# Attention and gated feed-forward on one core: softmax denominators summed by accumulating DMAs, and one PSUM bank for projections and transposes

## The chip, the cores and the metric

The kernel runs on one NeuronCore of a Trainium2 chip. Its engines are TensorE (PE in the profile: matrix products, with the loading of weights shown apart as PEld), VectorE (DVE), ScalarE (ACT), GpSimd (POOL) and SyncE (SP, which only starts transfers here). They run side by side and wait for each other through semaphores; each works through its own queue in order. Sixteen DMA engines move data; a transfer is started from the queue of SP, ACT or POOL. PE writes to PSUM, eight banks of 2 KB per partition, which ScalarE and VectorE read; everything else lies in SBUF or in HBM. The metric is the device time of the whole program in microseconds (us).

## The reference, cut to what matters

The input x has 4 batches of 1024 rows of 512 floats. Two layers follow each other, each with a layer norm before and after:

```python
x = x + layernorm(attention(layernorm(x)))
x = x + layernorm(ffn(layernorm(x)))

def attention(x):                       # 16 heads of 32
    kqv = x @ Wqkv + bqkv               # named q, k, v in this order
    scores = einsum('bsnh,btnh->bnst', k, q) / sqrt(32)
    scores = triu(scores) - 10000 * tril(ones, -1)
    attn = softmax(scores, axis=2)
    out = einsum('bnkq,bknh->bqnh', attn, v)
    return out.reshape(b, s, 512) @ Wo + bo

def ffn(x):                             # 2048 hidden units, int32 weights less 128, scaled per row
    return (silu(x @ Wg.T) * (x @ Wu.T)) @ Wd.T
```

A masked score is -10000, not minus infinity, and the scores are normalised over axis 2. For each query the kernel needs the maximum, the sum of exponentials (the denominator), and the sum of exponentials times values.

## The kernel before, in words

The first part of the program is attention, the second the feed-forward layer (`ffn`), which is not changed except for what is loaded ahead of it.

**Steps, tiles, periods.** Heads are taken four at a time (a block, `hb`, of 128 columns), queries 512 at a time (`g`, 0 or 1). One `(b, hb, g)` is a *step*; there are 32. A step goes over its key tiles `c` of 128 keys: four for `g` = 0, eight for `g` = 1. The last four tiles of a step lie on the diagonal, and only 512, 384, 256 and 128 queries of them count. Each key tile is a *period* of the big loop (from line 756), 192 in all, plus a lead of 12 in which the maxima of the first steps are found.

**A period.** PE's order is written out by hand. In period `p` the loop emits, for each half `u` (two heads), the scores of tile `now` (`weights`, L350 and L358 into `st`; ScalarE's exponential into `pT`, L375; on the diagonal GpSimd's mask, L377) and the maxima of a tile 12 periods ahead (`maxima`: PE into `sc`, L265; VectorE's L273 and L277). Between the halves stand, for the tile before: the accumulating transfers (`add_up`), one entry of a list called `later` (GpSimd's and VectorE's small products of steps already done), and `values` (L394), which multiplies `pT` with the values into `po` and with ones into `pd`, the denominators. Then comes one piece of a list called `whole`, or else one piece of a projection; at the period's end `fill` adds more projections.

**The planner.** Projections (`project`: q, k and v, four pieces each of 256 rows, and `project_out`) wait in lanes with a cost, a due period and a condition; `rate` and `spare` spread them over the periods. `whole` holds unsplit pieces: `rows` (`shift_rows`, which transposes the maxima into `pm`, and `masked_part`, which makes the masked keys' share in `pb` and `t1`), `ln` (stages of the layer norm) and `turn` (`turn_v`: transposes of v into `pv`).

**Denominators.** For `g` = 1 (but not the last step), the tiles 0 to 4 are added in SBUF: tile 0's `pT` is the sum tile, and each next is added to it by an accumulating DMA from GpSimd's queue (L421, two of 512 KB, one per half). The sum and the three narrow tiles 5 to 7 are multiplied by ones near the end of the step. For `g` = 0, each of the four tiles is multiplied by ones.

**PSUM.** `ps_st` has one buffer of two banks for scores, `ps_big` two buffers of two banks for maxima, for the second half of the scores where both halves are emitted together, and for every projection and transposition, `ps_acc` one bank each for `po` and `pd`: eight banks.

**Layer norm and emptying.** `ln_stage` loads, measures, normalises and transposes one row tile a stage; `xnT` holds a whole batch, double-buffered, and projections wait for all of it. ScalarE empties `xt` (L482), `pq` (L496, L499), `pm` (L305) and `pb` (L315); VectorE empties `pv` (L509) and `py` (L531) and adds the denominators (L446).

Of the kernel before, what the change touches and what calls it, by code (L numbers as in the profile page):

```python
# [27 lines left out]
def tile_attn_ffn_sandwich(  # L28
# [70 lines left out]
    with ExitStack() as actx:  # L99
# [3 lines left out]
        pxn = pctx.enter_context(tc.tile_pool(name="a_xn", bufs=2))  # L103
# [8 lines left out]
        ppt = right("a_pt", 6)  # L112
# [8 lines left out]
        )  # L121

# [103 lines left out]
        for step in steps:  # L226
            at[step] = n_periods
            n_periods += 4 * (step[2] + 1)
        LEAD = 12
        state = {}  # L230
        later = []

# [62 lines left out]
        def shift_rows(step):  # L295

            b, hb, g = step
            w = wide[g % 2]
            pm = ps_big.tile([P, 4, P], BF16, tag="big", name=f"pm_{b}_{hb}_{g}")
            for jj in range(4):  # L300
                nc.tensor.transpose(
                    pm[:, jj, :], w[:, jj].rearrange("p h d -> p (h d)"), ident_bf
                )
            mT = p2.tile([P, 512], BF16, tag="mT", name=f"mT_{b}_{hb}_{g}")
            nc.scalar.copy(mT, pm.rearrange("p j n -> p (j n)"))  # L305
            state["mT", step] = mT

        def masked_part(step):
# [3 lines left out]
            pb = ps_big.tile([P, 512], F32, tag="big", name=f"pb_{b}_{hb}_{g}")  # L312
            nc.tensor.matmul(pb, lhsT=sel, rhs=mT, start=True, stop=True)
            t1 = e2.tile([P, 512], F32, tag="t1", name=f"t1_{b}_{hb}_{g}")
            nc.scalar.activation(t1, pb, AF.Exp, bias=masked)  # L315
# [14 lines left out]
            later.extend((counts, shared))  # L330
            state["extra", step] = t1, t2

        def summed(step):

            return step[2] > 0 and step != steps[-1]

        def weights(step, c, halves):
# [27 lines left out]
            for u in halves:  # L365


                to_sum = summed(step) and c == 0
                pT = (p2 if to_sum else ppt).tile(
                    [P, 2, 512], F32, tag="sum" if to_sum else "pT",  # L370
                    name=f"pT_{b}_{hb}_{g}_{c}_{u}",
                )
                if to_sum:
                    state["sum", step, u] = pT
# [6 lines left out]
                state["pT", step, c, u] = pT  # L381

        def values(step, c):
            b, hb, g = step
            v = state["vt", b, hb]
            n = 512 * (g + 1) - max(c * P, 512 * g)
            first, last = c == 0, c == 4 * g + 3
            if first:
                for t in ("po", "pd"):
                    state[t] = ps_acc.tile([P, 512], F32, tag=t, name=f"{t}_{b}_{hb}_{g}")  # L390

            def product(t, pT, n, start, stop):
                for h in range(HPB):
                    nc.tensor.matmul(  # L394
                        state[t][h * D : (h + 1) * D, 512 - n :],
                        lhsT=v[:, c, h * D : (h + 1) * D] if t == "po" else ones,
                        rhs=pT[h // 2][:, h % 2, :n],
                        start=start,
                        stop=stop,
                    )  # L400

            pT = [state["pT", step, c, u] for u in range(2)]
            if not summed(step):
                product("pd", pT, n, first, last)
            product("po", pT, n, first, last)
            if summed(step) and c > 4 * g:

                waiting = state.setdefault(("pd", step), [])
                waiting.append((pT, n))
                if c > 4 * g + 1:  # L410
                    if c == 4 * g + 2:
                        total = [state.pop(("sum", step, u)) for u in range(2)]
                        waiting.insert(0, (total, 512))
                    for k, (t, n) in enumerate(waiting):
                        product("pd", t, n, c == 4 * g + 2 and k == 0, last)
                    waiting.clear()

        def add_up(step, c, u):

            if summed(step) and 0 < c <= 4 * step[2]:  # L420
                nc.gpsimd.dma_start(  # L421
                    state["sum", step, u], state["pT", step, c, u], accum_op=ALU.add
                )

        def finish(step):
# [6 lines left out]
            t1, t2 = state.pop(("extra", step))  # L432
            if step == steps[-1]:
# [12 lines left out]
            nc.vector.tensor_tensor(t2, state["pd"], t2, ALU.add)  # L446
            nc.vector.tensor_tensor(t1, state["po"], t1, ALU.add)

# [26 lines left out]
        def ln_turn(b, j):  # L475
            if j == 0:
                state["xnT", b] = pxn.tile([P, HC, S], F32, tag="xnT", name=f"xnT_{b}")
            xn = state.pop(("xn", b, j))
            pt = ps_big.tile([P, HC, P], F32, tag="big", name=f"xt_{b}_{j}")
            for c in range(HC):  # L480
                nc.tensor.transpose(pt[:, c, :], xn[:, ts(c, P)], ident)  # L481
            nc.scalar.copy(state["xnT", b][:, :, ts(j, P)], pt)  # L482

        def project(b, hb, which, q):

            xnT = state["xnT", b]
# [5 lines left out]
            pq = ps_big.tile([P, 256], F32, tag="big", name=f"pq_{b}_{hb}_{which}_{q}")  # L492
            by_columns(pq, [(w_in[which, hb][:, c, :], xnT[:, c, ts(q, 256)]) for c in range(HC)])
# [7 lines left out]
        def turn_v(b, hb, half):  # L501
# [4 lines left out]
            pv = ps_big.tile([P, 4, P], F32, tag="big", name=f"pv_{b}_{hb}_{half}")  # L506
            for i in range(4):
                nc.tensor.transpose(pv[:, i, :], vT[:, ts(4 * half + i, P)], ident)
            nc.vector.tensor_copy(state["vt", b, hb][:, 4 * half : 4 * half + 4, :], pv)  # L509
# [11 lines left out]
        def project_out(b, j, half):  # L521
# [5 lines left out]
            py = ps_big.tile([P, 256], F32, tag="big", name=f"py_{b}_{j}_{half}")  # L527
# [32 lines left out]
        def load_raw(k, which):  # L560
            raw = []
            for what, src in zip(which, weight_blocks(k)):
                shape = [P, IB // P, H] if what == "d" else [P, HC, IB]
                pool = pre["stage_d" if what == "d" else "stage"]
                t = pool.tile(shape, I32, tag=f"raw_{what}", name=f"raw_{what}{k}")
                nc.sync.dma_start(t, src)
                raw.append(t)
            return raw

        def ffn_begin():  # L570
# [11 lines left out]
            pre["stage_d"] = actx.enter_context(tc.tile_pool(name="a_raw", bufs=1))  # L582
            for i in range(GT):
                nc.sync.dma_start(pre["rows"][:, i, :], x2[0, i * P : (i + 1) * P, :])
            pre["raw"] = load_raw(0, "gud")
# [4 lines left out]
        def ffn_stage(i):  # L590
# [3 lines left out]
            if i > 0:  # L594
                xn = state.pop(("xn2", i - 1))
                pt = ps_big.tile([P, HC, P], F32, tag="big", name=f"xt2_{i - 1}")
                for c in range(HC):
                    nc.tensor.transpose(pt[:, c, :], xn[:, ts(c, P)], ident)
                hi, lo = (pre[k][:, :, ts(i - 1, P)] for k in ("hi", "lo"))
                nc.scalar.copy(hi, pt)  # L600
                nc.vector.tensor_tensor(lo, pt, hi, ALU.subtract)  # L601
# [4 lines left out]
            if i < 3:  # L606
                k = "gud"[i]
                nc.vector.tensor_scalar_add(pre[k], pre["raw"][i], -ZERO_POINT)
            if i == 3:
                pre["raw"] = load_raw(1, "gu")  # L610

        def check_weights():

            pf = ps_big.tile([P, P], F32, tag="big", name="pf")
# [36 lines left out]

        def turn_piece(b, hb, half):
# [420 lines left out]
```

## Time and profile before

| | |
|---|---|
| Time, median of 3 runs | 1977.89 us (1974.43 to 1981.7) |
| The profiled execution | 1978.49 us, its span 1976.4 us |
| Granted TensorE clock, mean over the span | 0.991 |
| First and last product of `values` | 80.4 and 1234.5 us |
| In 81 to 1235 us, busy | PE 1096.8, VectorE 797.5, ScalarE 442.0, GpSimd 426.2 us |
| Accumulating transfers | 120 of 512 KB, median 5.9 us from issue to landing |

How to read the profile's rows: a group is named by its line, engine, operation and `out<-in`; then come the shape, the count after `x`, the busy time and mean length of one, and the idle time of the engine before it with what ended it. In a row of the waits, "A <- B: total, times, longest" says how long A stood still until B ended. A timeline row gives start and length in us, and the idle time before it in brackets. A float32 product is recorded as two matmuls, so the four heads of one `pd` group are eight. The ends of matmuls are modelled and overlap the next start; what a group takes is read from start to start. In the slices, each digit is the busy share of a fortieth of the span in tenths, and PEclk the granted clock.

### The profile page before, as it was taken

How to read it: one execution, taken by the hardware profiler on the slowest of the kernel's cores; microseconds unless marked ns; L12 is line 12 of the kernel's file. 1: busy time of each engine (PE TensorE's matmuls, PEld its weight loads, DVE VectorE, ACT ScalarE, POOL GpSimd, SP SyncE). 2: the span in 40 equal slices, each digit the busy share in tenths (PEclk: the TensorE clock that was granted, in tenths of full speed). 3: DMA queues.
4: the chain of work that ended last, by engine and by line, in shares of the span. 5: the costliest groups of instructions: out<-in, count | busy, mean ns of one | idle time of the engine just before them, and what ended most of it. 6: DMA issues, size and time to landing. Idle time of an engine off the chain costs nothing.

```text
span 1976.4 us, 42103 instructions
## 1 busy us (share of the span) xinstructions
PE 1889.4 (96%) x18241; PEld 1121.0 (57%) x18241; DVE 1171.8 (59%) x1913; ACT 643.3 (33%) x962; POOL 524.3 (27%) x896
## 2 busy tenths in 40 slices
PE   7999999999999999999999989999999999999997
PEld 4444444444443444444444434688888888888886
DVE  4678777786675677675666773554344444444444
ACT  2244344434423434423344323122222222222221
POOL 2134233243343244344233344201010101101011
PEclk9999999999999999999999999999999999999999
DMA  3164255344235144144144351531010101001000
GB/s 113 55 145 100 68 121 126 77 118 97 50 87 114 27 98 92 39 103 92 23 87 86 98 129 50 175 108 43 1 44 0 43 6 38 32 11 43 0 22 23
DMA packets 65633, 137.56 MB, mean 70 GB/s; under 512 B 6304, under 2 KB 20640, under 8 KB 65440
## 3 DMA queue, kind: packets, MB, share of 16 engines
q0 software_dynamic: 17280, 62.92, 17.2%
q1 hardware_dynamic: 41008, 67.40, 10.1%
q10 hardware_dynamic: 7152, 4.46, 0.7%
q8 instruction: 145, 2.38, 0.5%
q14 instruction: 48, 0.39, 0.1%
HBM read 55.07 MB, written 16.78 MB: 36 GB/s over the span
## 4 chain that ended last, share of the span: by engine, by line
PE 82%; DVE 10%; ACT 4%; issue 2%; POOL 2%; DMA 1%; DVEq 0%; POOLq 0%; ACTq 0%; SPq 0%
PE pq L237 16%; PE pg L915 11%; PE pu L915 11%; PE acc L948 11%; PE sc L265 8%; PE po L394 5%; PE py L237 4%; PE st L350 4%; PE pd L394 4%; PE st L358 3%; DVE nm L277 3%; ACT pT L375 3%; DVE vl L516 2%; DVE sc L273 1%; PE xt L481 1%
## 5 line engine op out<-in xcount | busy, mean ns | idle before, releaser
L375 ACT ACTIVATE pT<-st 128x1024 f32<-128x1024 f32 (+3 forms) x384 | 310.2, 811 | 406.5 <-PE st L358 307.6
L277 DVE TENSOR_REDUCE nm<-sc 128x2 f32<-128x1024 f32 (+3 forms) x384 | 367.2, 957 | 117.5 <-PE st L358 98.2
L237 PE MATMUL pq<-xnT,w 128*32 128x256 f32 x6144 | 373.7, 386 | 16.1 <-DVE nm L277 6.8
L265 PE MATMUL sc<-in,in 32*128 32x512 f32 (+3 forms) x1536 | 347.8, 537 | 13.3 <-DVE nm L277 13.0
L237 PEld LDWEIGHTS pq<-xnT,w 128*32 128x32 f32 x6144 | 188.4, 111 | 218.4 <-issue 48.2
L358 PE MATMUL st<-in,in 32*128 32x512 f32 (+3 forms) x1536 | 308.7, 490 | 0.0
L925 DVE SCALAR_TENSOR_TENSOR h<-pu,pre_us,s 128x512 f32<-128x512 f32 x128 | 96.1, 750 | 312.8 <-PE pu L915 309.9
L377 POOL TENSOR_SCALAR_AFFINE_SELECT pT<-pT 128x256 f32<-128x256 f32 x256 | 113.5, 445 | 446.4 <-ACT pT L375 445.8
L948 PE MATMUL acc<-d,h 128*128 128x512 f32 x896 | 224.8, 393 | 0.2 <-DVE h L935 0.2
L273 DVE TENSOR_TENSOR sc<-sc,bound 128x256 f32<-128x256 f32 x256 | 109.2, 426 | 169.3 <-PE sc L265 96.6
L948 PEld LDWEIGHTS acc<-d,h 128*128 128x128 f32 x896 | 166.1, 188 | 34.2 <-DVE h L935 0.5
L923 ACT ACTIVATE s<-pg,pre_gs 128x512 f32<-128x512 f32 x128 | 88.1, 688 | 274.8 <-PE pg L915 274.7
L394 PE MATMUL po<-pT,vt 128*32 128x512 f32 (+3 forms) x1536 | 166.5, 502 | 1.0 <-POOL pT L377 1.0
L934 ACT CAST h<-h 128x512 fp32r<-128x512 f32 x128 | 79.5, 621 | 247.3 <-DVE h L925 247.3
L350 PE MATMUL st<-mT,ones_bf 3*128 3x512 bf16 (+3 forms) x768 | 125.9, 334 | 22.5 <-ACT pT L375 22.1
L935 DVE TENSOR_TENSOR h<-h,h 128x512 fp32r<-128x512 f32 x128 | 88.6, 692 | 88.0 <-ACT h L934 88.0
L358 PEld LDWEIGHTS st<-in,in 32*128 32x128 f32 x1536 | 135.5, 191 | 1.2
L265 PEld LDWEIGHTS sc<-in,in 32*128 32x128 f32 x1536 | 115.6, 184 | 34.4 <-PE st L358 11.7
L350 PEld LDWEIGHTS <-ones_bf 3*128 3x128 bf16 x768 | 40.8, 91 | 163.2 <-issue 159.1
L237 PE MATMUL py<-wo_sb,o 128*32 128x256 f32 x2048 | 122.0, 381 | 8.8 <-DVE pre_lo L601 1.9
L79 POOL TENSOR_SCALAR rs_y<-mv_y 128x1 f32<-128x1 f32 x32 | 8.7, 271 | 448.1 <-DVE mv_y L77 448.1
L499 ACT ACTIVATE in<-pq,b_sb 128x256 f32<-128x256 f32 x128 | 60.7, 474 | 194.5 <-PE pq L237 192.4
(135 smaller groups left out, 2581.5 us busy)
## 6 DMA issues: line engine op xcount, KB each, us to landing
pT<-pT POOLq DMA_DIRECT2D x120, 512.0 KB, 5.9
xr<-in_x SPq DMA_DIRECT2D x32, 256.0 KB, 3.4
xo<-in_x SPq DMA_DIRECT2D x32, 256.0 KB, 2.7
x<-xo SPq DMA_DIRECT2D x32, 256.0 KB, 2.0
out<-y SPq DMA_DIRECT2D x32, 256.0 KB, 2.0
look<-in_gate_wt SPq DMA_DIRECT2D x16, 256.0 KB, 3.8
look<-in_up_wt SPq DMA_DIRECT2D x16, 256.0 KB, 3.0
look<-in_down_wt SPq DMA_DIRECT2D x16, 256.0 KB, 2.9
```

Source lines behind the costliest of these rows:

```text
L237: nc.tensor.matmul(out[k * D : (k + 1) * D, :], lhsT=lhsT[:, k * D : (k + 1) * D], rhs=rhs, start=(c == 0), stop=(c == len(pairs) - 1),)
L265: nc.tensor.matmul(sc[:, h % 2, :n], lhsT=qT[h * D : (h + 1) * D, ts(j, P)], rhs=kT[h * D : (h + 1) * D, 512 * k : 512 * k + n], start=Tru ...
L273: nc.vector.tensor_tensor(sc[:, :, n - P : n], sc[:, :, n - P : n], bound.unsqueeze(1).to_broadcast((P, 2, P)), ALU.min,)
L277: nc.vector.tensor_reduce(nm[:, k, jj, 2 * u : 2 * u + 2], sc[:, :, :n], AX.X, ALU.max, negate=True)
L350: nc.tensor.matmul(st[h // 2][:, h % 2, :n], lhsT=ones_bf[h * D : h * D + 3, :], rhs=mT[h * D : h * D + 3, 512 - n :], start=True, stop=False,
L358: nc.tensor.matmul(st[h // 2][:, h % 2, :n], lhsT=kT[h * D : (h + 1) * D, ts(c, P)], rhs=qT[h * D : (h + 1) * D, q0 : q0 + n], start=False ...
L375: nc.scalar.activation(pT[:, :, :n], st[u][:, :, :n], AF.Exp)
L377: nc.gpsimd.affine_select(out=pT[:, :, :P], in_=pT[:, :, :P], compare_op=ALU.is_ge, fill=0.0, base=0, pattern=[[0, 2], [1, P]], channel_mu ...
L394: nc.tensor.matmul(state[t][h * D : (h + 1) * D, 512 - n :], lhsT=v[:, c, h * D : (h + 1) * D] if t == "po" else ones, rhs=pT[h // 2][:, h ...
L915: nc.tensor.matmul(dst, lhsT=w[i * P // IB][:, c, ts(i % (IB // P), P)], rhs=part[:, c, :], start=(c == 0 and k == 0), stop=(c == HC - 1 a ...
L925: nc.vector.scalar_tensor_tensor(h, pu, us_sb[:, i : i + 1], s, ALU.mult, ALU.mult)
L948: nc.tensor.matmul(acc[t0][t], lhsT=part[:, ts(t, P)], rhs=dw[i * P // IB][:, i % (IB // P), :], start=(i == 0 and k == 0), stop=(i == IC ...
```

## The change

- **Sums.** In every step but the last, all key tiles are added to the sum tile by accumulating DMAs: one transfer for all four heads (1 MB at 512 queries, less for the narrow ones), three for `g` = 0 and seven for `g` = 1. `pT` is now one tile of four heads with three buffers, `sum` has two buffers. One product with ones per step (`quotients`), two periods (`WAIT`) after the step's last tile, makes the denominators. The last step multiplies each tile by ones as before, the first two of them at the third.
- **One bank in two halves.** `pd` has no bank of its own. The bank is split into halves of 256 floats, taken in turn (`half_bank`) by projections, transposes, `pm`, `pb`, `py`; the denominators take both halves at once. What was 512 wide (`pb`, `xt`, `xt2`, `pv`) comes in two pieces, each emptied by itself. In the last step these take a buffer of `ps_big` again. Otherwise `ps_big` holds scores alone.
- **Layer norm by half batches.** `xnT` becomes tiles of half a batch with three buffers; a projection waits only for its half. The second half of a batch's transposes waits until the first two v pieces of the last head block of the batch before are out.
- **Order.** `counts` and `shared` go to the front of `later`; `rows` goes ahead of the other whole pieces; the second half of q and k is due four periods later; output projections become ready three periods later (`after - 4 + WAIT`, `after + 4 + WAIT`).
- **Loads ahead of the feed-forward.** Two staging buffers in turn take the places of three: down weights of block 0 are loaded when gate weights have been converted.

```diff
-        pxn = pctx.enter_context(tc.tile_pool(name="a_xn", bufs=2))
+        pxn = pctx.enter_context(tc.tile_pool(name="a_xn", bufs=3))
-        ppt = right("a_pt", 6)
+        ppt = right("a_pt", 3)
+        ps_half = actx.enter_context(
+            tc.tile_pool(name="a_half", bufs=1, space=bass.MemoryType.PSUM)
+        )
+        halves_of = ps_half.tile([P, 2, 256], F32, tag="half", name="half_banks")
...
+        WAIT = 2
+        def half_bank(shape, name, dtype=F32):
+            if state.get("last"):
+                return ps_big.tile(shape, dtype, tag="big", name=name)
+            state["half"] = 1 - state.get("half", 1)
+            t = halves_of[:, state["half"], :]
+            if dtype == BF16:
+                t = t.bitcast(BF16)
+            if len(shape) == 3:
+                return t.rearrange("p (i n) -> p i n", i=shape[1])
+            return t[:, : shape[1]]
...
-            pb = ps_big.tile([P, 512], F32, tag="big", name=f"pb_{b}_{hb}_{g}")
-            nc.tensor.matmul(pb, lhsT=sel, rhs=mT, start=True, stop=True)
-            nc.scalar.activation(t1, pb, AF.Exp, bias=masked)
+            for k in range(2):
+                pb = half_bank([P, 256], f"pb_{b}_{hb}_{g}_{k}")
+                nc.tensor.matmul(pb, lhsT=sel, rhs=mT[:, ts(k, 256)], start=True, stop=True)
+                nc.scalar.activation(t1[:, ts(k, 256)], pb, AF.Exp, bias=masked)
...
-            later.extend((counts, shared))
+            later[:0] = (counts, shared)
...
+        def sums(pT, n, start=True, stop=True):
+            state["pd"] = halves_of.rearrange("p k n -> p (k n)")
+            for h in range(HPB):
+                nc.tensor.matmul(
+                    state["pd"][h * D : (h + 1) * D, 512 - n :],
+                    lhsT=ones,
+                    rhs=pT[:, h, :n],
+                    start=start,
+                    stop=stop,
+                )
+
+        def add_up(step, c):
+            if c > 0 and step != steps[-1]:
+                n = width(step, c)
                 nc.gpsimd.dma_start(
-                    state["sum", step, u], state["pT", step, c, u], accum_op=ALU.add
+                    state["sum", step][:, :, 512 - n :], state["pT", step, c][:, :, :n],
+                    accum_op=ALU.add,
                 )
...
+        def quotients(step):
+            b, hb, g = step
+            o = state["o", b, hb]
+            t1, t2 = state.pop(("quotients", step))
+            sums(state.pop(("sum", step)), 512)
+            for k in range(2):
+                t = t2[:, ts(k, 256)]
+                nc.vector.tensor_tensor(t, state["pd"][:, ts(k, 256)], t, ALU.add)
...
-            pt = ps_big.tile([P, HC, P], F32, tag="big", name=f"xt_{b}_{j}")
-            for c in range(HC):
-                nc.tensor.transpose(pt[:, c, :], xn[:, ts(c, P)], ident)
-            nc.scalar.copy(state["xnT", b][:, :, ts(j, P)], pt)
+            for k in range(2):
+                pt = half_bank([P, 2, P], f"xt_{b}_{j}_{k}")
+                for c in range(2):
+                    nc.tensor.transpose(pt[:, c, :], xn[:, ts(2 * k + c, P)], ident)
+                nc.scalar.copy(state["xnT", b, half][:, 2 * k : 2 * k + 2, ts(i, P)], pt)
...
-            pq = ps_big.tile([P, 256], F32, tag="big", name=f"pq_{b}_{hb}_{which}_{q}")
+            pq = half_bank([P, 256], f"pq_{b}_{hb}_{which}_{q}")
...
-            pv = ps_big.tile([P, 4, P], F32, tag="big", name=f"pv_{b}_{hb}_{half}")
-            for i in range(4):
-                nc.tensor.transpose(pv[:, i, :], vT[:, ts(4 * half + i, P)], ident)
-            nc.vector.tensor_copy(state["vt", b, hb][:, 4 * half : 4 * half + 4, :], pv)
+            for k in range(4 * half, 4 * half + 4, 2):
+                pv = half_bank([P, 2, P], f"pv_{b}_{hb}_{k}")
+                for i in range(2):
+                    nc.tensor.transpose(pv[:, i, :], vT[:, ts(k + i, P)], ident)
+                nc.vector.tensor_copy(state["vt", b, hb][:, k : k + 2, :], pv)
...
+                put(whole["ln"], 0, here - 24,
+                    lambda p, b=b, j=j, t=here - 46: p >= t and (
+                        j - 3 < NJ // 2 or b == 0 or emitted.get(("v", b - 1, HC - 1), 0) >= 2
+                    ),
+                    ln_stage, b, j)
...
+                        put(lanes["qk"], FULL, i - LEAD - 1 + (4 if q >= NQ // 2 else 0),
+                            lambda p, b=b, i=i, q=q: p >= i - 24 and normed(b, q),
...
-            ahead = heads(whole, p)
+            ahead = sorted(heads(whole, p), key=lambda h: h[1] != "rows")
...
+        ends = {at[step] + 4 * (step[2] + 1) + WAIT: step for step in steps[:-1]}
...
                 if u == 0:
+                    if p in ends:
+                        quotients(ends[p])
                     if before:
                         values(*before)
```

## The prediction

> **What bounds the kernel now.** I read the page first: its engine table, its slices and its chain.
>
> ```profile
> span 1976.4 us, 42103 instructions
> PE 1889.4 (96%) x18241; PEld 1121.0 (57%) x18241; DVE 1171.8 (59%) x1913; ACT 643.3 (33%) x962; POOL 524.3 (27%) x896
> PE   7999999999999999999999989999999999999997
> PEclk9999999999999999999999999999999999999999
> PE 82%; DVE 10%; ACT 4%; issue 2%; POOL 2%; DMA 1%; DVEq 0%; POOLq 0%; ACTq 0%; SPq 0%
> ```
>
> TensorE (PE) is at nine tenths in nearly every slice at full clock and carries 82% of the chain. A busy PE may hide pauses, so I looked at starts in the timeline of one step with four key tiles. Its denominators (pd, L394) stand directly before the next work:
>
> ```profile
> 510.67 0.85 PE L394 MATMUL pd<-pT,ones 128*32 128x384 f32 x8
> 511.33 0.83 PE L394 MATMUL po<-pT,vt 128*32 128x384 f32 x8
> 515.57 0.64 PE L394 MATMUL pd<-pT,ones 128*32 128x256 f32 x8
> 516.02 0.61 PE L394 MATMUL po<-pT,vt 128*32 128x256 f32 x8
> 522.78 0.43 PE L394 MATMUL pd<-pT,ones 128*32 128x128 f32 x8
> 523.02 0.40 PE L394 MATMUL po<-pT,vt 128*32 128x128 f32 x8
> ```
>
> From pd's start to po's start is what pd really occupies: 0.66, 0.45 and 0.24 us. Last, the waits of PE between 100 and 1290 us: 58 us over all lines, the largest being
>
> ```profile
> PE st L350 <- ACT pT L375: 20.6, 57, 0.8
> PE sc L265 <- DVE nm L277: 11.4, 14, 3.0
> PE pq L237 <- DVE nm L277: 5.1, 5, 1.4
> ```
>
> So attention (from 81 to 1235 us, 192 periods of 6.0 us each) is bound by PE; VectorE has 798 us busy in it, ScalarE 442, GpSimd 426. Any pause that the change puts between two PE instructions counts almost in full, and so does any product it removes.
>
> **What it removes.** Every step but the last loses its three narrow pd groups (384, 256 and 128 queries) and keeps one of 512: 0.66 + 0.45 + 0.24 = 1.35 us, 31 times: **-42 us**. Score tiles no longer share their two buffers with projections. The waits of sc, pq and py for the maxima (11.4 + 5.1 + 1.8 us) then mostly go: **-18 us**. Together -60. The largest wait, st for the exponential, has its own buffer and stays.
>
> **What it adds on PE: one bank for everything small.** Projections, transposes, the masked row (pb) and the denominators now share one bank. A rule of the Trainium skill speaks against this: "PSUM — Partial Sum Buffer", section "PSUM bank collisions raise a hardware error", says that accesses of two engines to one bank and 32-partition quadrant collide even at different addresses, so they must be guarded by bank. If it holds, the two halves are no double buffer: PE may not write one half while ScalarE or VectorE reads the other. The trace has no such pair, but the start-up shows what a wait for one emptied tile costs:
>
> ```profile
> 9.52 5.78 PE L237 MATMUL pq<-xnT,w 128*32 128x256 f32 x64 [0.68 <-ACT xnT L482]
> L482 ACT COPY xnT<-xt x32: 586/586/588, 7.6 to 793.4; 128x512 f32<-128x512 f32 x32
> ```
>
> 0.68 us is the copy of 0.586 us plus 0.04 before and 0.05 after. For half width I take the copy as 0.38 (a ScalarE row of 256 elements, pT, takes 0.38), the projection's own emptying as 0.474 (its row, with 0.07 before it), the exponential likewise, and VectorE as 0.41 (py, 256 wide, takes 0.42). Then, by the rule:
> - pb in two halves: 0.04 + 0.47 + 0.05 = 0.57, 32 times: 18 us.
> - xt of the first layer norm in two: 0.47, 32 times: 15 us. xt2 in two, where both ScalarE and VectorE must read each half: 0.94, 4 times: 4 us.
> - pv in two: VectorE starts 0.2 us after the last transpose on the mean, being behind score tiles; 0.2 + 0.41 + 0.05 = 0.66, 32 times: 21 us.
> - Projections that follow one another with nothing between. PE's order has 28 doubles of pq and 7 of py; with a few more around the start-up some 36, at 0.07 + 0.47 + 0.05 = 0.6: 21 us.
> - The new denominator group. Two periods after its step it fills the whole bank; the next step's pb comes in the same period, behind the values product of 0.66 to 0.88 us. VectorE has about 0.4 us of maxima left when the group ends, then two additions of 0.41: 0.4 + 0.83 + 0.05 less about 0.8 is 0.5, 31 times: 16 us.
>
> That is **+95 us** by the rule. Without it (halves emptied independently) only the denominator's 16 would stay. I take the rule: nothing in the trace contradicts it. Where a score tile lies between two uses, PE has 0.5 to 1.1 us of other work and I cost nothing; that cover is thin in the 128-wide periods (0.45 us).
>
> **What it adds on GpSimd and the DMAs.** Before, 120 accumulations of 512 KB, two to a tile. Now 31 x 3 narrow ones, and 15 x 4 of 1 MB: 153. One sum tile takes all of a step's, so each waits on GpSimd for the one before to land, and behind that wait stand the second mask (L377) of the running tile, the products of `later` and the next step's masks. The rows:
>
> ```profile
> pT<-pT POOLq DMA_DIRECT2D x120, 512.0 KB, 5.9
> q0 software_dynamic: 17280, 62.92, 17.2%
> L421 POOL DMA_DIRECT2D pT<-pT x120: 852/878/1220, 107.1 to 1158.6; - x120
> DMA to landing us min/median/max: 4.6/5.9/10.2
> ```
>
> 17.2% of 16 engines is 5439 us for 120 transfers, 45 us each, 2.83 us on 16 engines; the shortest landing, 4.6 us, leaves 1.8 outside. A transfer of 1 MB is then 1.8 + 5.6 = 7.4 us; those of 384, 256 and 128 queries about 6.1, 4.7 and 3.4. "DMA: Bandwidth & Descriptors", section "Anatomy of one DMA — SWDGE (gpsimd) path", fits 2.0 us plus bytes over 436 GB/s, 4.4 us for 1 MB: less than half a landing would fit a period of 6.0 us comfortably, and nothing would be late. The row decides: an accumulation already takes 4.6 us for half of that, so 7.4 exceeds a period.
>
> I laid this over the trace's own times. In the eight-tile step whose exponentials of tiles 1 to 7 end at 247.5, 253.1, 258.6, 264.4, 270.6, 276.1 and 282.2 us, transfers start at 247.5, 254.9, 262.3, 269.7, 277.1, 283.2 and 287.9; the last lands at 291.3. The denominator is due at about 294.9, so it has 3 us of slack. But tile 6's second mask stands behind the transfer issued at 277.1: plus 0.88 of issue and 0.41 of mask it is ready at 278.4, and its values product started at 276.5. PE waits about 1.9 us there. The same arithmetic over all steps, each delay carried on to what follows, gives 19 us with 7.2 us for a large transfer, 25 with 7.4 and 35 with 7.7. I take **+25 us**. No buffer of weights is late by more than 1 us in sum, and no denominator.
>
> Unknown is the issue of a narrow transfer, which has 512 rows where the measured one had 128. Its price lies between nothing more than 0.88 us and four times that (+2.6 us, 93 times, all beside the masks): the overlay then gives 135 us instead of 19. A gain is excluded. I take nothing, since 0.88 is the only row, and keep 135 for the range.
>
> **Edits that I cost at nothing.** Doubled emptyings add 0.1 to 0.3 us each to ScalarE and VectorE, which have 700 and 350 us free in this stretch. Layer norm by halves and its waits move pieces by a few periods, ahead of their due ones; the cover is the 11 periods before the batch's first use. Down weights loaded two periods later land in about 5.6 us, and 12 us are there; uncovered, 5.6 us once. `py` ready three periods later near the end: the PE still has the same work.
>
> **Sum.** -60 + 95 + 25 = 60. Some pauses will fall where PE already waits for exponentials (20.6 us); half of that, 10, is taken off: +50. On the profiled execution's 1978.5 us (span 1976.4 and 2.1 around it, within 0.03% of the 1977.89 median) that is **2028 us**. A half per cent (10 us) is about what a measurement of this kernel can tell from no change.
>
> **Rivals.** (1) *The halves do work apart, or the pauses sink into each other*: a PE pause lets GpSimd and the transfers catch up. With 16 of the 95 and a few us of late masks, 1978 - 60 + 22 = 1940: faster. For it speaks that PE's waits and GpSimd's lateness are added here as though independent. It decides if the pauses of one bank stay under some 35 us. (2) *Issue of narrow transfers becomes the bound*: 512 rows cost four times 128. 2028 + 135 - 25 = 2138, or near 2115 with overlap. Against it: large parts of 0.88 us may not depend on rows. (3) *Gain and price cancel*: half the pauses hidden, 1978 - 60 + 47 + 12 = 1977; the change then only moves PE's work into waits.
>
> **Chances.** The sum as above 0.52 (own range 1990 to 2070), rival 1 0.20, rival 2 0.14, rival 3 0.14. Slower: 0.52 + 0.14 and a little of rival 3, 0.69; faster 0.21; same 0.10. The range takes in most of rival 1 and the near part of rival 2: 1938 to 2105.
>
> **What would show it.** pd falls from 1056 to 312 matmuls; q0 moves 112 MB. Right: between the halves of pb, pv and xt, PE idle of 0.5 to 0.7 us put down to ScalarE or VectorE; GpSimd waiting on its own transfers in nearly every tile; po waiting for pT's mask, some 25 us. Wrong: such halves back to back; narrow issues well above 0.88 us; landings of 1 MB under 6 us; PE waits in attention not much above 58 us.

## The result, and the profile after

The changed kernel takes **2151.5 us** (2147.4 to 2152.9), where the one before took 1978.8 us beside it: a ratio of 1.087, with an interval of 1.085 to 1.090, or 173 us more. The forecast was slower by 50. The direction was right, and the size was short by 123 us.

The page of the changed kernel, its engine table and two rows of its slices:

```profile
span 2150.4 us, 40491 instructions
PE 1905.2 (89%) x17529; PEld 1088.7 (51%) x17529; DVE 1184.1 (55%) x1980; ACT 658.7 (31%) x1030; POOL 588.9 (27%) x929
PE   6888888888887898898978887799999999999997
PEclk9899999999899999999999998999999999999999
```

PE has 712 instructions fewer (17529 for 18241), and yet its busy time grew from 1889.4 to 1905.2 us. The slices place the change: up to the twenty-sixth, PE mostly stands at 8 or 7 where it stood at 9. The feed-forward part behind is as it was. What is lost, then, is lost before its first product (pg), which starts at 1427.0 us where it started at 1252.3. The view by stretches gives that part in one line for each kernel. Its columns are the stretch, its length, the busy time of PE, PEld, DVE, ACT and POOL with their counts, the granted clock, the DMA share and GB/s. Before:

```profile
0.00:1252.00 1252.00, 1177.81 (x15057) 533.60 (x15057) 860.71 (x1390) 461.05 (x677) 446.55 (x784) 0.99 0.39 88
```

and after:

```profile
0.00:1427.00 1427.00, 1193.84 (x14345) 501.22 (x14346) 872.55 (x1458) 477.73 (x746) 511.31 (x817) 0.94 0.56 111
```

Length less PE's busy time is its idle time: 74 us before, 233 after, 159 more of the 175. The second item is the clock, 0.94 for 0.99. Followed through short windows of the trace, it isn't a little low everywhere: it is full nearly throughout and **half** in single stretches, 8 of them before (31 us together), 30 after (167 us together). In such stretches a projection's matmul takes 97 ns from start to start, elsewhere 51, so the work takes about twice as long. Half their length, 15 and 84 us, is then an estimate of what they cost; as PE stood idle for 29 us of those after, 69 is nearer there. PE's busy time hides that second item: groups gone or shortened (denominators 80.2 to 34.6 us from start to start, maxima 167.0 to 127.7) are outweighed by others that stretched (projections' columns 480.8 to 525.9, values 148.8 to 170.1).

What PE waits for in the changed kernel, by line (total, times, longest):

```profile
PE po L415 <- POOL pT L392: 67.2, 36, 5.0
PE half_banks L545 <- DVE vt L546: 29.7, 32, 2.4
PE half_banks L333 <- ACT t L334: 18.3, 31, 0.6
PE st L365 <- ACT pT L390: 17.0, 42, 0.8
PE half_banks L515 <- ACT xnT L516: 16.7, 36, 0.5
PE half_banks L333 <- DVE t L477: 14.3, 29, 3.2
PE half_banks L631 <- DVE pre_lo L636: 10.0, 4, 4.4
...
PE half_banks L255 <- ACT in L535: 6.3, 12, 0.6
```

Every row named half_banks is the one bank: pieces that wait until the piece before is emptied. The largest row is another, a wait for masks. In the kernel before, the waits for masks were these, 3 us in all:

```profile
PE pd L394 <- POOL pT L377: 2.0, 2, 1.0
PE po L394 <- POOL pT L377: 1.0, 1, 1.0
```

Behind the masks stand the transfers, here in the page's parts on queues, groups and DMA issues:

```profile
q0 software_dynamic: 57744, 111.68, 30.5%
...
L440 POOL DMA_DIRECT2D pT<-pT x153 | 176.4, 1153 | 333.9 <-DMA pT<-pT 299.5
...
pT<-pT POOLq DMA_DIRECT2D x60, 1024.0 KB, 7.7
pT<-pT POOLq DMA_DIRECT2D x31, 768.0 KB, 7.3
pT<-pT POOLq DMA_DIRECT2D x31, 512.0 KB, 5.5
...
pT<-pT POOLq DMA_DIRECT2D x31, 256.0 KB, 4.4
```

GpSimd stood still for 299.5 us until its own last transfer had landed, 88 times. Before, it was 30.8 us:

```profile
L421 POOL DMA_DIRECT2D pT<-pT x120 | 106.8, 941 | 55.5 <-DMA pT<-pT 30.8 <-ACT pT L375 11.1 <-ACT in L499 7.0
```

A narrow issue takes 1.30 us (the median over its own instructions), a wide one 0.88. One case of such a wait, in the timeline of an eight-tile step (start, length, and in brackets the idle time before and what ended it):

```profile
471.69 0.94 POOL L440 DMA_DIRECT2D pT<-pT  x1 [3.63 <-DMA pT<-pT]
...
473.97 0.40 POOL L392 TENSOR_SCALAR_AFFINE_SELECT pT<-pT 128x256 f32<-128x256 f32 x1
...
474.43 1.39 PE L415 MATMUL po<-pT,vt 128*32 128x384 f32 x4 [2.53 <-POOL pT L392]
...
480.90 1.36 POOL L440 DMA_DIRECT2D pT<-pT  x1 [5.74 <-DMA pT<-pT]
```

GpSimd waits 3.63 us for the transfer before, issues the next, works off three small pieces, and only then comes to the mask; PE has waited 2.53 us for it. Then look at the length of the product: the four matmuls of 384 recorded take 1.39 us, where eight of that width took 0.83 in the timeline before. The stretch that begins there:

```profile
474.60:481.40 6.80, 6.34 (x46) 2.43 (x46) 2.59 (x6) 1.34 (x3) 1.06 (x3) 0.50 0.99 227
```

The granted clock is 0.50 for 6.8 us. PE is busy for 6.34 us of it, by the same estimate with work worth half that. The wait of 2.53 us has then cost another 3.2.

### The profile page after: what moved, and what is told of

Read it like the earlier page. It is cut to its first block, busy times and chain, and to the rows that moved or that the text cites. A ratio compares the mean times of both kernels' runs of the same rounds, so it can differ in the third digit from the quotient of the medians.

```text
span 2150.4 us, 40491 instructions
## 1 busy us (share of the span) xinstructions
PE 1905.2 (89%) x17529; PEld 1088.7 (51%) x17529; DVE 1184.1 (55%) x1980; ACT 658.7 (31%) x1030; POOL 588.9 (27%) x929
## 5 line engine op out<-in xcount | busy, mean ns | idle before, releaser
L255 PE MATMUL half_banks<-xnT,w 128*32 128x256 f32 x6144 | 408.8, 406 | 17.3 <-ACT in L532 8.1
L283 PE MATMUL sc<-in,in 32*128 32x512 f32 (+3 forms) x1536 | 356.6, 555 | 5.0 <-DVE nm L295 5.0
L373 PE MATMUL st<-in,in 32*128 32x512 f32 (+3 forms) x1536 | 318.3, 505 | 0.0
L255 PEld LDWEIGHTS half_banks<-xnT,w 128*32 128x32 f32 x6144 | 193.5, 116 | 246.5 <-issue 62.4
L440 POOL DMA_DIRECT2D pT<-pT x153 | 176.4, 1153 | 333.9 <-DMA pT<-pT 299.5
L415 PE MATMUL po<-pT,vt 128*32 128x512 f32 (+3 forms) x1536 | 191.5, 504 | 73.2 <-POOL pT L392 67.2
L392 POOL TENSOR_SCALAR_AFFINE_SELECT pT<-pT 128x256 f32<-128x256 f32 x256 | 129.3, 533 | 365.9 <-ACT pT L390 365.8
L415 PEld LDWEIGHTS po<-pT,vt 128*32 128x32 f32 x1536 | 40.2, 109 | 199.4 <-POOL pT L392 91.0
L535 ACT ACTIVATE in<-half_banks,b_sb 128x256 f32<-128x256 f32 x128 | 60.7, 474 | 216.9 <-PE half_banks L255 214.9
```

What stands on the lines that cost most here:

```text
L255: nc.tensor.matmul(out[k * D : (k + 1) * D, :], lhsT=lhsT[:, k * D : (k + 1) * D], rhs=rhs, start=(c == 0), stop=(c == len(pairs) - 1),)
L283: nc.tensor.matmul(sc[:, h % 2, :n], lhsT=qT[h * D : (h + 1) * D, ts(j, P)], rhs=kT[h * D : (h + 1) * D, 512 * k : 512 * k + n], start=Tru ...
L373: nc.tensor.matmul(st[h // 2][:, h % 2, :n], lhsT=kT[h * D : (h + 1) * D, ts(c, P)], rhs=qT[h * D : (h + 1) * D, q0 : q0 + n], start=False ...
L392: nc.gpsimd.affine_select(out=pT[:, :, :P], in_=pT[:, :, :P], compare_op=ALU.is_ge, fill=0.0, base=0, pattern=[[0, 2], [1, P]], channel_mu ...
L415: nc.tensor.matmul(state["po"][h * D : (h + 1) * D, 512 - n :], lhsT=v[:, c, h * D : (h + 1) * D], rhs=pT[:, h, :n], start=(c == 0), stop= ...
L440: nc.gpsimd.dma_start(state["sum", step][:, :, 512 - n :], state["pT", step, c][:, :, :n], accum_op=ALU.add,)
```

## Experiments

Ratios are to the kernel before, whose median lay between 1975.4 and 1976.2 us in these batches. "Idle" and "half clock" are PE's idle time before pg and the length of its half-clock stretches together, as above.

**The two large parts apart.** One kernel takes the bank away: every small piece has a buffer of `ps_big` again, pd keeps the bank for itself, the pieces stay cut in two.

```diff
-            if state.get("last"):
+            if True:
                 return ps_big.tile(shape, dtype, tag="big", name=name)
```

> The changed kernel, but projections, transposes, pb and pm take the two buffers of ps_big again (the pieces stay 256 wide), and the denominators have the bank alone. Theory (pauses of the one bank, late masks and half clock add up): the pauses after emptyings, some 125 us of PE idle in the changed kernel, fall to the 30 us or so of the kernel before; the masks stay late (67 us or a little more, since PE leaves the transfers less time); half clock falls from 84 us lost to about 55: 2020 to 2045 us. Rival A (the accumulations alone do the harm, the bank is harmless): no more than 20 us gained, above 2130. Rival B (the bank alone does it): within 30 us of the kernel before less its 42 us of products, below 1970.

The other takes the transfers away, so that the sums hold only the first tile:

```diff
-            if c > 0 and step != steps[-1]:
+            if False:
                 n = width(step, c)
                 nc.gpsimd.dma_start(
```

> The changed kernel without any accumulating transfer: the sums leave out all key tiles but the first, so no accumulation stands in GpSimd's queue; everything else, the denominators' product too, stays. Theory: PE's wait for masks (67 us) goes to the 3 us of before, the half clock's loss falls from 84 to about 45, the bank's pauses stay: 2035 to 2065 us. Rival A: 1940 to 1970. Rival B: above 2120.

and the third takes both away:

> Both edits at once: own buffers for the small pieces, and no accumulating transfer (the sums leave out all key tiles but the first). What is left of the change is the products that are gone. Theory: the half clock comes back to about 15 us lost as before and PE's idle time to about 60 us, so the kernel before less 42 us of products and some waits for maxima: 1925 to 1950 us. If the half clock has another cause than PE's pauses (rival C), it stays at 84 us lost and the time is near 2000.

| | with transfers | without |
|---|---|---|
| pieces in halves of one bank | 2151.5 | 2027.2 (1.026, 1.023 to 1.029) |
| pieces in buffers of their own | 2098.2 (1.062, 1.060 to 1.063) | 1970.9 (0.997, 0.996 to 0.998) |

The two parts add up: the transfers cost 124 or 127 us, the bank 53 or 56. None of the three times lies in the range expected for it: the bank gave back 53 us instead of 106 to 131, the kernel without transfers is 8 us faster than its range, and the one without both is 21 us slower, about what the cutting of the pieces is worth there (23 us, below). The larger part of the loss is that of the transfers, which the forecast had put at 25, less an absorption of 10. How they cost so much shows when the two middle kernels are read together. With the bank and no transfers:

```profile
0.00:1301.00 1301.00, 1136.25 (x14345) 485.99 (x14345) 852.89 (x1457) 476.65 (x746) 336.22 (x664) 0.98 0.12 36
```

With transfers and no shared bank:

```profile
0.00:1383.00 1383.00, 1232.27 (x14346) 538.62 (x14347) 883.32 (x1458) 473.53 (x746) 515.64 (x817) 0.95 0.58 115
```

PE is idle 165 us in the first and 151 in the second: the first idles *more*. But its idle time is mostly of pauses of half a microsecond, and its half clock is 55 us in all; in the second the masks are late by up to 5.7 us at a time, its half clock is 147 us, and the same instructions keep PE busy for 1232 us instead of 1136. Not all of these 96 us are the clock's, though, since own buffers without transfers have 1164 already:

```profile
0.00:1249.00 1249.00, 1164.17 (x14345) 512.77 (x14345) 854.84 (x1457) 472.26 (x746) 339.14 (x664) 0.98 0.12 38
```

In either row of the table, then, the transfers lengthen PE's busy time, by 58 us with the one bank and by 68 with own buffers. Half of PE's busy time at half clock, the estimate of what the clock costs, grows by 44 and 51; what the rest is isn't traced.

**Transfers at another place in the order.** If masks are late because they stand behind a waiting transfer, a transfer issued when its forerunner has landed should cost nothing. They go into a list and are issued half a period to a whole one later:

```diff
-                if before and u == 0:
-                    add_up(*before)
+                if before and u == 0 and before[1] > 0:
+                    g, c = before[0][2], before[1]
+                    due = (p + 1, 0) if c > 2 else (p, 1 if c == 2 or g == 0 else 0)
+                    adds.append((due, before))
+                while adds and adds[0][0] <= (p, u):
+                    add_up(*adds.pop(0)[1])
```

> The changed kernel with the same transfers put later in GpSimd's queue: those of tile 1 (short steps) and tile 2 half a period later, of tile 3 and later a whole period, about where they start anyway because each waits for the one before. Theory (the masks are late because they stand behind a transfer that waits for the one before): PE's wait for masks falls from 67 to under 20 us, with some half clock: 2060 to 2100 us. Rival D (masks are late since GpSimd or the DMA engines are too full, whatever the order): within 20 us of the changed kernel, or slower because the last sum lands after the denominators are due.

2217.2 us, 1.123 (1.121 to 1.126): slower still, the second outcome that rival D names. The wait for masks went from 67.2 to 5.3 us as meant, and PE waits for these instead:

```profile
PE st L366 <- ACT pT L391: 59.9, 64, 3.9
PE half_banks L429 <- DMA pT<-pT: 48.7, 14, 6.8
```

Scores now wait for exponentials, which wait (127 us, where it was 12) for one of the three pT buffers, read by a transfer still under way; and the denominators wait for the end of the sums, up to 6.8 us. Half clock: 239 us. So another order by itself is no cure. The chain of an eight-tile step takes 4 x 7.7 + 7.3 + 5.5 + 4.4 = 48 us of landings, and the step lasts eight periods of 6.0 us in the kernel before. There is no slack to move. Later denominators together with more buffers for pT were not tried.

**Cutting pieces in two.** Of the kernel with buffers of its own and no transfers, one version undoes the cutting of pb, xt, xt2 and pv; here xt for all:

```diff
-            for k in range(2):
-                pt = half_bank([P, 2, P], f"xt_{b}_{j}_{k}")
-                for c in range(2):
-                    nc.tensor.transpose(pt[:, c, :], xn[:, ts(2 * k + c, P)], ident)
-                nc.scalar.copy(state["xnT", b, half][:, 2 * k : 2 * k + 2, ts(i, P)], pt)
+            pt = half_bank([P, HC, P], f"xt_{b}_{j}")
+            for c in range(HC):
+                nc.tensor.transpose(pt[:, c, :], xn[:, ts(c, P)], ident)
+            nc.scalar.copy(state["xnT", b, half][:, :, ts(i, P)], pt)
```

> The kernel own_bank_no_adds (own buffers for the small pieces, no accumulating transfer, so the sums leave out all key tiles but the first), with pb, xt, xt2 and pv in one piece again as before. It gained only 5 us on the kernel before where 42 us of products are gone. Theory: twice as many pieces turn the two shared buffers faster, and maxima and weights on PE lose some 15 us and the transposes 12 us inside rows that look busy: 1935 to 1950 us here. Rival E (the products that are gone were covered by something else, and never on the path): 1965 to 1975.

1947.6 us, 0.985 (0.983 to 0.988). Two others keep the one bank but hand it out whole, with the pieces undivided:

```diff
-            state["half"] = 1 - state.get("half", 1)
-            t = halves_of[:, state["half"], :]
+            t = halves_of.rearrange("p k n -> p (k n)")
             if dtype == BF16:
-                t = t.bitcast(BF16)
+                t = t[:, :256].bitcast(BF16)
```

> The changed kernel with the one bank used whole: pb, xt, xt2 and pv in one piece each, every piece at the bank's start. Transfers as in the changed kernel. Theory (the halves are no double buffer, so cutting a piece in two only adds a pause between its halves): the pauses inside pairs go, about 18 us for pb, 17 for xt, 24 for pv, 5 for xt2, and little of the half clock: 2075 to 2105 us. Rival F (the halves do double-buffer; the pauses have other causes): the same as the changed kernel or slower, 2145 to 2190.

> The kernel whole_bank (one bank, pieces undivided) without any accumulating transfer; the sums leave out all key tiles but the first. With transfers, undivided pieces gained 45 us where the pauses inside pairs were some 64. Theory (the masks took back what the pauses gave, because a PE that does not pause leaves the transfers less time): without transfers the whole of it shows against no_adds (2027): 1958 to 1972 us. If the pauses are simply worth 45, about 1982.

Without transfers the whole bank takes 1949.7 us (0.987, 0.984 to 0.989), no more than buffers of its own. The two in that order, the whole bank second:

```profile
0.00:1223.00 1223.00, 1143.94 (x14315) 508.93 (x14316) 850.46 (x1422) 461.58 (x678) 342.99 (x664) 0.98 0.12 39
0.00:1225.00 1225.00, 1110.67 (x14313) 482.17 (x14313) 845.00 (x1420) 462.11 (x678) 343.14 (x664) 0.98 0.12 39
```

PE idles 35 us longer (114 for 79) and is busy 33 us less: the maxima, alone with scores in `ps_big`, take 127 us from start to start instead of 170, while the scores' own products take 230 instead of 212. It is the **cutting** in one bank that costs: 2027.2 less 1949.7 is 77 us. (With own buffers, cutting costs 23.) Both times of the whole bank lie just outside their ranges, this one 8 us below, the one with transfers 2 above. With transfers only 45 of the 77 come back (2106.6 us, 1.066, 1.064 to 1.068), and the waits for masks grow from 67.2 to 86.0. That a PE which pauses less leaves the transfers less time would explain it:

```profile
PE po L413 <- POOL pT L390: 86.0, 45, 5.3
```

**Wide and narrow transfers apart.** One kernel leaves the narrow tiles out of the sums, one the wide ones:

```diff
-            if c > 0 and step != steps[-1]:
+            if 0 < c <= 4 * step[2] and step != steps[-1]:
```

> The changed kernel without the 93 narrow transfers: the sums leave out the tiles on the diagonal after the first of them, and the 60 of 1 MB stay. Theory (the masks are late because the narrow transfers stand in line behind the wide ones, and in front of the masks): only the mask of the tile after the wide chain can be late; PE's wait for masks falls from 67 to under 15 us and most of the half clock with it: 2035 to 2065 us, near the 2027 without any. Rival G (the wide transfers carry the price): above 2110.

```diff
-            if c > 0 and step != steps[-1]:
+            if c > 4 * step[2] and step != steps[-1]:
```

> The changed kernel with the 93 narrow transfers alone; the 60 of 1 MB are left out, and so tiles 1 to 4 of a long step from the sums. Theory (the narrow transfers, in line behind the wide ones, stand before the masks): without the wide ones before them each narrow chain starts on time and only the last tiles' masks wait, so the two kinds cost less apart than together: no_narrow is 14 us over no_adds, this 20 to 50 us over it, 2045 to 2075, against 124 for both. Rival I (the narrow ones do it by themselves): above 2110.

With the wide ones alone 2041.1 us (1.032, 1.029 to 1.035), with the narrow ones alone 2074.3 (1.049, 1.045 to 1.052). Over the 2027.2 of none that is 14 and 47 us; both together are 124. The waits for masks go the same way, 67.2 us with both, and with the wide ones and the narrow ones alone:

```profile
PE po L415 <- POOL pT L392: 7.6, 10, 1.7
PE po L415 <- POOL pT L392: 22.1, 19, 5.5
```

The rest, 63 us, is there only with both kinds. That the narrow ones then queue up behind the wide ones in the second half of an eight-tile step, where the masks are, fits this; it isn't followed step by step. The narrow ones alone make masks late although their chain, 17 us, is shorter than any step; the first landing of that chain, 7.3 us, is already longer than a period of 6.0.

**What a late mask costs by itself.** In the kernel *before*, with nothing of the change, the second mask of the third diagonal tile is applied ten times, which leaves the values as they are and makes it late by some 3.7 us in each step:

```diff
-                if c >= 4 * g:
+                for _ in range(10 if c == 4 * g + 2 and u == 1 else c >= 4 * g):
```

> The kernel before, with nothing of the change, but the second mask of the third diagonal tile of every step is applied ten times over (the same zeros again). Nine more at 0.41 us make it 3.7 us later; by the trace of before the values product has 0 to 4 us of slack there, so PE should wait some 70 us in 31 places, as long as the changed kernel's PE waits for its masks (67 us in 36), with no transfer and no bank involved. Theory (such pauses of 2 us and more let the clock fall to half, which costs about as much again): half clock rises from 15 us lost to 45 or more, and the time by 100 to 140 us: 2075 to 2115. Rival C (the half clock of the changed kernel has another cause): 15 to 25 us lost, 2035 to 2055.

2106.3 us, 1.066 (1.064 to 1.068): 130 us more. Its stretch before pg, and its waits for masks:

```profile
0.00:1384.00 1384.00, 1230.51 (x15059) 548.11 (x15060) 862.92 (x1391) 461.09 (x677) 562.65 (x1072) 0.96 0.35 80
```

```profile
PE po L394 <- POOL pT L377: 45.8, 16, 3.9
PE pd L394 <- POOL pT L377: 35.3, 19, 2.9
```

PE idles 153 us, 79 more than before; the two rows sum to 81. The half clock grew from 31 to 116 us, and PE was idle for 14 of these, so that some 36 us of work more are lost by the estimate used above. Idle and clock make 115 of the 130; the rest isn't traced. So late masks alone, without one more transfer and without the bank, bring on the half clock, and with it a wait costs 1.6 times its length (130 us for 81).

**Two versions meant to beat the kernel before.** Both have own buffers, undivided pieces, complete sums, and eight-tile steps summed nearly as before (tiles 0 to 4 by transfers, one a tile in the first version and two in the second; the narrow ones by ones products); only the four-tile steps, which before had no transfers, get one ones product. In the first GpSimd adds their tiles itself, in the second three narrow transfers do:

```diff
+            if c > 0 and step[2] == 0:
+                n = width(step, c)
+                part = state["sum", step][:, 2 * u : 2 * u + 2, 512 - n :]
+                nc.gpsimd.tensor_tensor(
+                    part, part, state["pT", step, c][:, 2 * u : 2 * u + 2, :n], ALU.add
+                )
```

> An attempt at a version that beats both: own buffers, pieces undivided, long steps summed as before the change (one transfer of 1 MB for tiles 1 to 4, narrow tiles by ones products), short steps summed by GpSimd itself (two additions a tile, one per half, about 2.2 us per 1024 elements by the rows of its products) and one ones product. 16 x 1.35 = 22 us of products gone. Theory: GpSimd has the time, the additions of 0.6 to 1.7 us delay a mask by no more than PE's slack: 1950 to 1972 us. Rival H (masks come late behind the additions too, and the clock with them): 1985 or above.

```diff
+            if step[2] == 0 and c > 0:
+                nc.gpsimd.dma_start(total[:, :, 512 - n :], pT[:, :, :n], accum_op=ALU.add)
```

> A version that might beat both: own buffers, undivided pieces, long steps summed as before the change (two transfers of 512 KB a tile for tiles 1 to 4, narrow tiles by ones products), short steps by their three narrow transfers and one ones product two periods later. 16 x 1.35 = 22 us of products gone. Theory (no backlog of wide transfers ahead of these, so masks are late by a few tenths only): 1952 to 1970 us. If a chain of three narrow transfers alone already holds masks back: 1985 or more.

2040.2 us (1.032, 1.029 to 1.035) and 2043.3 us (1.035, 1.032 to 1.038): neither beats it, and both miss their ranges. In the second, masks are late again (30.4 us, up to 5.6) although only short steps changed, and the half clock is 106 us. In the first, PE waits little for masks (8.1 us), so its time is rival H's without rival H's mechanism. It waits 34 us for VectorE's maxima, 14.9 for their shifts, and 15.2 for transfers of the long steps that the denominators need. Of VectorE's 128 small shift operations, 26 took 0.6 to 1.2 us instead of some 0.2; all of these ran beside additions or multiplications of GpSimd, but 24 others that ran beside its additions stayed short. No run here separates this from the mere order of work, so the cause stays open for this kernel.

## Why the prediction was right or wrong

The runs form a chain from the kernel before to the changed one, to set beside the sum's terms:

| step | predicted | measured |
|---|---|---|
| ones products gone (1976 to 1947.6) | -42 | -28 |
| pieces cut, in halves of one bank, and scores alone in theirs (1947.6 to 2027.2) | -18 + 95 = +77 | +80 |
| transfers (2027.2 to 2151.5) | +25 - 10 = +15 | +124 |

**Products: the mechanism right, the size nearly.** The denominators' own time fell by 46 us from start to start (forecast 42). Of the kernel's time 28 came off: PE idles 5 us more, the half clock grew from 31 to 41 us (some 4 us of work, by estimate), and the remaining 9 aren't traced. Layer norm by half batches and the new order are in this 28 as well; they weren't tried by themselves.

**One bank: the mechanism right, the sum in part by luck.** The pauses, measured against forecast: pb 18.3 (18), xt 16.7 (15), pv 29.7 (21), xt2 10.0 (4), denominators behind VectorE's additions 14.3 (16), projections in succession 8.1 + 6.3 + 6.2 = 20.6 (21). Together 110 for 95. Two of the terms, pv and xt2, were too small, it seems because VectorE got to the piece later than taken. The relief was short too: PE's idle time grew by 86 (79 to 165), so 24 us of other waits went, for 18. Besides, the maxima's own time fell by 43 (170 to 127), which no term foresaw, but PE's busy time by only 7, as scores, projections and the cut pieces took longer; why isn't traced. So 80 for 77 comes of errors that cancel. The halves are no double buffer in this program, as the rule of the Trainium skill ("PSUM — Partial Sum Buffer", section "PSUM bank collisions raise a hardware error") led the forecast to take; whether the chip or only the program's own guards forbid it, no run here tried. **Rival 1** needed these pauses under 35 us and falls with them.

**Masks behind transfers: the step that failed.** "I take **+25 us**" named the right wait at the right place, but the term was mis-sized in two ways. First, its durations: 7.4, 6.1, 4.7 and 3.4 us were taken for the landings, and 7.7, 7.3, 5.5 and 4.4 were measured; 0.88 us for a narrow issue, and 1.30 was measured. With these in place of the others the same overlay gives some 48 us, by estimate; the profile shows 67. The overlay itself had warned: 7.2, 7.4 and 7.7 us gave 19, 25 and 35, so the chain was about as long as its step. The remaining 19 us aren't traced one by one. Second, and larger, a whole term was missing: a wait on PE was charged its own length. The transfers brought 68 us of idle time (165 to 233) and kept PE busy 58 us longer with the same instructions (1136 to 1194); together these are the 124, within 2. Of the 58, some 44 are half clock by the estimate above (stretches of 55 us became 167), and 14 aren't traced. The delayed mask, on the kernel before, brings on the same without the change.

**Absorption of 10: not seen.** Over the whole span, waits for exponentials only fell from 22.1 to 17.0 us. The parts added up as though independent, and with the whole bank the reverse was seen: fewer pauses made masks later.

**Rival 2** ended nearest to the measured time (2138), by the wrong mechanism: it needed a narrow issue of 3.5 us. The price of 1.30 is 39 us of GpSimd's time over 93 issues, part of the 48 above. **Rival 3** falls with rival 1.

**Costed at nothing, rightly:** the end of the sums. The overlay gave the denominator 3 us of slack, and in the changed kernel PE waited for it 0.4 us in all; delaying the transfers by up to a period used this slack up (48.7 us).

**Was there anything to win?** The kernels that sum nothing at all take 1947.6 and 1949.7 us. In this arrangement, then, the change had at most some 28 us to give, and the transfers put 124 on the other side.

## What to carry to other kernels

Where a chain of accumulations in an in-order queue lasts as long as the step it belongs to, or one landing longer than a period, look at what stands behind each link in that queue; moving the links only moved the wait here. Price the waits of TensorE with the half clock that may follow: add up its idle time in stretches of some 3.4 us. Where late masks brought these sums above some 1.6 us, a wait cost 1.6 to 1.8 times its length; many scattered waits of half a microsecond cost little more than theirs (the bank's 80 us of them lost some 8 us of clock, by estimate). In this program two halves of one PSUM bank are no double buffer: whole pieces in one bank cost nothing net here, the same pieces cut in two cost 77 us.

## What the runs showed of the hardware that was not expected

The forecast said nothing of the clock. In the changed kernel's trace, the changes of the granted clock before pg lie whole multiples of 3.41 us apart, and the stretches at 0.50 lasted 3.4, 6.8, 10.2 or 13.7 us. What goes with a fall is less the length of one wait than PE's idle time added up over one such stretch of 3.41 us: ahead of the 30 falls it was 1.56 to 3.35 us, and of the 334 such stretches at full clock (from 15 us to pg) that no fall followed, five had that much, at most 1.88. Ahead of 22 falls a single wait of 2 us or more reached into the stretch; but three near the start (at 20.6, 30.8 and 41.1 us) came after pauses of 0.46 to 0.60 us that made 1.66 together. Over all fourteen traces, 144 of 145 such stretches with 2 us or more of idle time were followed by half clock, and 17 of 4562 with less than 1.25.

The Trainium skill, "TensorE: Matmul & The Clock Gate", section "HAM oscillation — how this bites in real kernels", lets no gap above about 3.4 us stand; by that, the 2.53 us wait shown above would have gone free, and it was followed by 6.8 us at half clock. The length of the stretches agrees with that page, whose section "What's actually happening" states a window of 3413 ns; the shortest harmful wait doesn't agree with the rule on gaps.

Accumulating packets had a price of their own: on the mean 660 ns for 8192 bytes, but 153, 112 and 73 ns for 1536, 1024 and 512, so that a byte of the smallest costs 1.8 times one of the largest. For 512 packets on 16 engines that is 4.9, 3.6 and 2.3 us; with the 1.8 us outside that the forecast took, 6.7, 5.4 and 4.1 by estimate, most of the way from the 6.1, 4.7 and 3.4 forecast to the landings measured.
